# Four stacked graph layers on one core: both graphs' messages in one VectorE instruction, node copies and a positive part on ScalarE

## The chip, the cores and the metric

The kernel runs on one core of a Trainium2 chip. The metric is the device time of one execution in microseconds, lower is better. The engines are named as in the profile: PE is TensorE (PEld its weight loads), DVE is VectorE, ACT is ScalarE, POOL is GpSimd, SP is SyncE. SBUF is the on-chip working memory, PSUM the memory of eight banks per partition that PE writes its results into.

## The reference

There are 128 graphs of 64 nodes, with 128 features per node (`x`) and a 64 x 64 weighted adjacency (`adj`). Four layers follow each other; each adds its result to `x` and normalizes over the features. Layers 0 and 1 are continuous-filter convolutions over edges, layers 2 and 3 are graph convolutions over the whole adjacency.

```python
def ssp(x): return softplus(x) - log(2)

# layer 0 (20 Gaussians); layer 1 is alike with 64 Gaussians and the mask A = adj
f = exp(coeff * (d_ij[..., None] - offsets)**2)        # one row per edge (i, j)
y = x @ w_in2f
W = (ssp(f @ fw1 + fb1) @ fw2 + fb2) * rcut[..., None] # the filter of an edge
agg = einsum('bjf,bijf->bif', y, W)                    # sum of messages per node
x = layernorm(x + ssp(agg @ ow1 + ob1) @ ow2 + ob2)

# layer 2
h = elu(elu(x @ W0 + b0));  h = elu(norm_A @ (h @ W1) + b1)
x = layernorm(x + norm_A @ (h @ W2) + b2)
# layer 3
x = layernorm(x + relu((A_norm @ x) @ W.T + b))
```

## The kernel before

The kernel has a sparse path and a dense one; the sparse one runs here. It sorts the graphs and their nodes by degree, keeps only the nonzero entries of `adj`, and packs them into fixed lists of slots, so that two graphs (a pair) always have the same layout. A prelude of some 85 us does the first part of this; the rest of the packing is spread over the first layer as background work (`early`, `side`), mostly on DVE and POOL.

**The main loop** goes over 64 pairs in layer 0 and 64 in layer 1, each cut into three chunks, so 192 iterations per layer. A chunk holds 316 to 364 slots of each of the two graphs in layer 0 and 380 to 420 in layer 1. For chunk `c` the steps are:

- `filter_in`: PE multiplies the Gaussians `d` with the first filter matrix into the PSUM tile `px` (two banks, one per graph), and ACT takes `h = exp(px + b1)`. `softplus`: ACT takes `h = ln(0.5 h + 0.5)`.
- `gather`: PE multiplies node features `ys` with the one-hot rows `hot` (made on DVE in `one_hot`) into `pg` (two banks); ACT copies it to `g` in SBUF.
- `filter_out`: PE multiplies `h` with the second filter matrix into `pw`, one matmul per graph (each shown as two passes).
- `message`: DVE computes `m = (pw + b2) * g`. After the third chunk of a pair `slot_sums` adds the messages of every node on DVE (lines 1828 and 1832), four such sums at a time in the following iterations.

The loop is skewed by hand: iteration `i` does `filter_in` of chunk `i`, `gather` of chunk `i-1`, and `filter_out` and `message` of chunk `i-2`. The order on each engine is that in which the program issues (`in_order` ties it). Cut down, an iteration is

```python
run(sums, (1, 4, 4)[k]); run(early, ...); run(side, ...)
...
filter_in(c)
gather(c1)
softplus(c)
slot(nodes)                 # one step of node work, every queue in turn
filter_out(c2)
message(c2)
slot(convs[0])
gaussians(n + 1, k)
slot(convs[1])
```

**PSUM** has eight banks: two for `px`, two for `pg`, two for `pw`, and two for node work (`ps_n`, taken in turn by `bank`). `px` and `pg` have one buffer each. `pw` has two buffers of one bank, so that graph 0 of a chunk takes one bank and graph 1 the other, and each bank is free again when its own message has been taken. `g` has two buffers in SBUF, `h` three.

**Node work** is done for groups of four pairs (512 columns), in queues of generators that give one step per `slot`. `node_before` transposes `x` (line 1429), copies it to `xt` (line 1432, DVE), multiplies it with the input matrix, and copies the result to `ys` on ACT. `node_after` multiplies the sums with the first output matrix into `u`, and computes a softplus as `max(u + c1, 0) + ln(0.5 exp(-|u + c1|) + 0.5)`: `na` on ACT (Abs, Exp, Ln) and the positive part `nh` on DVE (line 1558), added on DVE (line 1566); two more matmuls and a normalization follow. `graph_convs` does layers 2 and 3 of a group while layer 1 still runs, with copies from PSUM by `copy` (line 1637: `gxt`, `gy_hw`, `gy_sup`), on DVE, and for the last few groups (`at_end`) on ACT. All activations go by the helper `act` (line 950).

Of the kernel before, what the change touches and what calls it, by code (L numbers as in the profile page):

```python
# [12 lines left out]
F32 = mybir.dt.float32  # L13
AF = mybir.ActivationFunctionType
ALU = mybir.AluOpType
AX = mybir.AxisListType
PSUM = bass.MemoryType.PSUM
DRAM = bass.MemoryType.DRAM

P = 128  # L20
# [581 lines left out]
def sparse_stack(ctx: ExitStack, tc: tile.TileContext, t: dict, out: bass.AP, flag):  # L602
# [11 lines left out]
    nc = tc.nc  # L614
# [155 lines left out]
    for b in range(2):  # L770
        for k in range(3):
            at = slice(A * b + NG0 * k, A * b + NG0 * (k + 1))
            nc.scalar.dma_start(fw1[at, k, :], t["L0_gnn_fw1"])
        at = slice(A * b, A * b + 3 * NG0)
# [101 lines left out]
    with (  # L876
# [31 lines left out]
        to = const.tile([NB, 1], U32, name="graph_to")  # L908
# [18 lines left out]
    node = ctx.enter_context(tc.tile_pool(name="snode", bufs=2))  # L927
    ps_x = ctx.enter_context(tc.tile_pool(name="sps_x", bufs=1, space=PSUM))
    ps_g = ctx.enter_context(tc.tile_pool(name="sps_g", bufs=1, space=PSUM))
    ps_w = ctx.enter_context(tc.tile_pool(name="sps_w", bufs=2, space=PSUM))  # L930


    compacting = ctx.enter_context(ExitStack())
# [5 lines left out]
    def act(out_, in_, func, **kw):  # L939
        nonlocal fence, latest, kind  # L940
        now = func == AF.Sin
        if kind is None or now != kind:
            fence = latest
            if not now:
                ctx_ = tc.issue_after(fence.ins) if fence is not None else nullcontext()
                with ctx_:
                    fence = nc.scalar.preload_act_table_set("natural_log_exp_and_others")
            kind = now
        with tc.issue_after(fence.ins) if fence is not None else nullcontext():
            latest = nc.scalar.activation(out_, in_, func, **kw)  # L950
        return latest
# [407 lines left out]
    g = {}  # L1359
# [12 lines left out]
    def bank(name, n=GS):  # L1372
        ps = ps_n.tile([P, 512], F32, tag="n", name=name)[:, 0 : n * P]
        return ps, ps.rearrange("p (s c) -> p s c", s=n)

    def by_pair(v):
        return v.rearrange("p (s c) -> p s c", c=P)
# [11 lines left out]
    def once(name, n, q):  # L1389

        if n < GS and rings:
            return tiled(name, n, q)
        return node.tile([P, GS * P], F32, tag=name, name=f"{name}_{q}", bufs=1)[:, 0 : n * P]
# [27 lines left out]
    def node_before(layer, q):  # L1421

        w = layers[layer]
        name = f"{layer}_{q}"
        xs = x_all[:, GROUPS[layer][q], :]
        n = xs.shape[1]
        flat, ps = bank(f"xT_{name}", n)
        for s in range(n):
            nc.tensor.transpose(ps[:, s, :], xs[:, s, :], ident)
        yield True  # L1430
        xt = node.tile([P, 512], F32, tag="xt", name=f"xt_{name}", bufs=1)[:, 0 : n * P]
        nc.vector.tensor_copy(xt, flat)

        nc.gpsimd.tensor_tensor(xs, xs, w["c2"].unsqueeze(1).to_broadcast([P, n, C]), ALU.add)
        yield
        flat, ps = bank(f"y_{name}", n)
        for s in range(n):
            nc.tensor.matmul(
                ps[:, s, :], lhsT=xt[:, s * P : (s + 1) * P], rhs=w["win"], start=True, stop=True
            )  # L1440
        yield True
        y = node.tile([P, n, C], F32, tag=f"y{n}", name=f"ys_{name}", bufs={GS: 3, 2: 1, 1: 2}[n])
        act(y, ps, AF.Copy)
        feats[layer, q] = y
        yield


    w = layers[0]
# [4 lines left out]
    u = ps_n.tile([P, 512], F32, tag="n", name="zero_x")  # L1453
# [4 lines left out]
    u = ps_n.tile([P, 512], F32, tag="n", name="zero_w")  # L1458
# [42 lines left out]
    def zero_share(q, agg):  # L1501

        n = agg.shape[1]
        rows = zero_rows.pop(q)
        for b in range(2):
            at = slice(b * A, (b + 1) * A)
            nc.vector.tensor_scalar(zblk[at, :, at], rows[at], 0.0, None, ALU.is_equal)
        yield
        _, ps = bank(f"zT_{q}", n)
        for s in range(n):  # L1510
            nc.tensor.transpose(ps[:, s, :], zblk[:, s, :], ident)
        yield True
        zt = by_pair(once("zt", n, q))
        act(zt, ps, AF.Copy)
        yield
        _, ps = bank(f"zs_{q}", n)
        y = feats[0, q]
        for s in range(n):
            nc.tensor.matmul(ps[:, s, :], lhsT=y[:, s, :], rhs=zt[:, s, :], start=True, stop=True)
        yield True  # L1520
        nc.vector.scalar_tensor_tensor(agg, ps, zero_filter, agg, ALU.mult, ALU.add)
        yield
# [15 lines left out]
    def node_after(layer, q, agg):  # L1538


        w = layers[layer]
        name = f"{layer}_{q}"
        n = agg.shape[1]
        codes = node_codes.pop((layer, q))
        if layer == 0:
            yield from zero_share(q, agg)
        elif n == GS:
            yield
        u, _ = bank(f"u_{name}", n)
        nc.tensor.matmul(  # L1550
            u, lhsT=w["o1"], rhs=agg.rearrange("f s r -> f (s r)"), start=True, stop=True
        )
        yield True
        a = once("na", n, q)
        act(a, u, AF.Abs, bias=w["c1"])
        act(a, a, AF.Exp, scale=-1.0)
        h = once("nh", n, q)
        nc.vector.tensor_scalar(h, u, w["c1"], 0.0, ALU.add, ALU.max)
        yield
        act(a, a, AF.Ln, scale=0.5, bias=half)  # L1560

        back = once("bk", n, q)
        nc.vector.tensor_scalar(back, codes, row[:, 0:1], None, ALU.is_equal)
        back = by_pair(back)
        yield
        nc.vector.tensor_add(h, h, a)
        yield
        _, ps = bank(f"o_{name}", n)
        for s in range(n):
            nc.tensor.matmul(  # L1570
                ps[:, s, :], lhsT=h[:, s * P : (s + 1) * P], rhs=w["o2"], start=True, stop=True
            )
        yield True
        o = by_pair(once("no", n, q))
        act(o, ps, AF.Copy)
        yield
        _, ps = bank(f"back_{name}", n)
        for s in range(n):
            nc.tensor.matmul(ps[:, s, :], lhsT=back[:, s, :], rhs=o[:, s, :], start=True, stop=True)
        yield True  # L1580
        y = by_pair(once("ny", n, q))
        xs = x_all[:, GROUPS[layer][q], :]
        nc.vector.tensor_add(y, ps, xs)
        yield
        yield from layernorm(y, xs, n, name)
        if layer == 1:
            if n < GS:
                yield from graph_convs(q)
            else:
                convs[q % 2].append(graph_convs(q))  # L1590
# [40 lines left out]

    def copy(to, ps, q):

        if q in at_end:
            act(to, ps, AF.Copy)
        else:
            nc.vector.tensor_copy(to, ps)

    normals = {}

# [11 lines left out]
    def graph_convs(q):  # L1652
# [5 lines left out]
        def times(name, lhs, rhs):  # L1658

            _, ps = bank(f"{name}_{q}", n)  # L1660
            for s in range(n):
                nc.tensor.matmul(ps[:, s, :], lhsT=lhs(s), rhs=rhs(s), start=True, stop=True)
            yield True
            y = by_pair(tiled(f"gy_{name}", n, q))
            copy(y, ps, q)
            yield
            return y
# [102 lines left out]
        act(c["h"], c["h"], AF.Ln, scale=0.5, bias=half)  # L1770

    def filter_out(c):
        c["pw"] = []
        for b in range(2):
            ps = ps_w.tile([P, 512], F32, tag="w", name=f"pw_{c['id']}_{b}")
            nc.tensor.matmul(  # L1776
                ps[:, 0 : c["size"]], lhsT=c["w"]["w2"], rhs=c["h"][:, b, :], start=True, stop=True
            )
            c["pw"].append(ps)

    def gather(c):

# [14 lines left out]
    def message(c):  # L1797
        n, k, size = c["n"], c["k"], c["size"]
        if k == 0:
            m = work.tile([P, 2 * MAX_SLOTS], F32, tag="m", name=f"m_{n}")  # L1800
            messages[n] = m[:, 0 : 6 * size].rearrange("f (b k) -> f b k", b=2)
        at = slice(k * size, (k + 1) * size)
        for b in range(2):
            nc.vector.scalar_tensor_tensor(  # L1804
                messages[n][:, b, at], c["pw"][b][:, 0:size], c["w"]["b2"], c["g"][:, b, :],
                ALU.add, ALU.mult,
            )
        if k == 2:
            sums.append(slot_sums(c, messages.pop(n)))

# [31 lines left out]
    at_end = range(NP // GS - 2, len(GROUPS[1]))  # L1842
    last = {q: deque() for q in small_groups}
    stores = deque()
    slot_data, messages, aggs = {}, {}, {}
# [61 lines left out]
    for i in range(3 * N + 2):  # L1907
        n, k = divmod(i, 3)
        c, c1, c2 = None, *past
# [19 lines left out]
        if n < N:  # L1929
            layer, p = pair_at(n)  # L1930
            q = next(q for q, group in enumerate(GROUPS[layer]) if group.start <= p < group.stop)
            c = dict(
                id=f"{n}_{k}", n=n, k=k, s=p - GROUPS[layer][q].start, at=(layer, q), w=layers[layer],
                size=CHUNKS[layer][p // 8],
            )
# [24 lines left out]
        if c2 is not None:  # L1960
            filter_out(c2)
            message(c2)
# [61 lines left out]
```

## Time and profile before

| | |
|---|---|
| median of 3 runs | 1656.86 us (1652.58 to 1659.53) |
| the profiled execution | 1684.44 us |
| its span, first to last instruction | 1682.6 us |
| PE busy | 1474.7 us (88%), 6813 matmul passes |
| DVE busy | 1481.3 us (88%), 4032 instructions |
| ACT busy | 1279.8 us (76%), 1723 instructions |
| POOL busy | 738.2 us (44%), 1180 instructions |
| mean granted clock of PE | 0.961 |

A row of the profile's groups names the line, the engine, the operation, what it writes and reads (`out<-in`), shapes, the count, then the busy time and the mean duration of one, then the engine's idle time just before such instructions and what ended it. A row of waits names who waited for whom, then the total in us, the number of waits and the longest. Layer 0's loop runs from about 95 to 803 us, layer 1's from 803 to about 1610 us, and then a tail of node work for the last groups.

### The profile page before, as it was taken

What the parts mean: (1) busy time and instruction counts of PE and PEld (TensorE: products, weight loads), DVE (VectorE), ACT (ScalarE), POOL (GpSimd) and SP (SyncE); (2) the same over time, 40 slices, a digit from 0 to 9 for tenths busy, and PEclk for the clock granted to TensorE, in tenths of its full rate; (3) what the DMA queues carried; (4) which work ended last, traced back from release to release, by engine and by line L of the source; (5) the groups of instructions that cost most, each with busy time, mean ns of one, the idle gap of its engine ahead of it and who ended that gap; (6) DMA issues with size and microseconds to landing.
All of it is one profiled execution on the core that took longest, in us unless ns stands there. A gap on an engine that the chain in (4) does not pass through costs nothing.

```text
span 1682.6 us, 24560 instructions
## 1 busy us (share of the span) xinstructions
PE 1474.7 (88%) x6813; PEld 816.6 (49%) x6813; DVE 1481.3 (88%) x4032; ACT 1279.8 (76%) x1723; POOL 738.2 (44%) x1180
## 2 busy tenths in 40 slices
PE   0177898999989989998999999999999999998976
PEld 0133454444545545555445555555555555554544
DVE  6677999999998999999888989999999989898874
ACT  1166797878878878887999878888888888787742
POOL 2325155454554533443422355445455335454444
PEclk9999999999999999998999999999999999999975
DMA  7644364545545454444665555555555544466100
GB/s 243 187 113 112 93 142 119 136 121 134 129 108 123 112 136 111 117 114 116 154 154 134 132 118 134 140 121 127 135 122 126 133 119 111 112 141 138 43 8 22
DMA packets 122294, 205.70 MB, mean 122 GB/s; under 512 B 47957, under 2 KB 80035, under 8 KB 121507
## 3 DMA queue, kind: packets, MB, share of 16 engines
q1 hardware_dynamic: 110784, 187.61, 46.1%
q0 software_dynamic: 6576, 14.99, 2.7%
q10 hardware_dynamic: 4786, 1.43, 0.4%
q8 instruction: 57, 0.93, 0.2%
q14 instruction: 91, 0.74, 0.2%
HBM read 185.29 MB, written 18.64 MB: 121 GB/s over the span
## 4 chain that ended last, share of the span: by engine, by line
DVE 32%; PE 25%; DMA 12%; ACT 11%; POOL 9%; issue 7%; SPq 3%; another core or an unknown queue 0%; ACTq 0%; DVEq 0%; POOLq 0%
DVE m L1804 9%; PE pw L1776 9%; DMA out_dram<-gz,at_row 6%; PE px L1762 6%; ACT h L950 5%; DVE agg L1828 5%; PE pg L1789 4%; DVE hot L1750 4%; POOL gz L1413 2%; POOL x_all L1413 2%; SPq L1289 2%; DVE at L1178 2%; ACT g L950 2%; ACT d L950 2%; POOL rs L1408 2%
## 5 line engine op out<-in xcount | busy, mean ns | idle before, releaser
L950 ACT ACTIVATE g<-pg 128x672 f32<-128x672 f32 (+12 forms) x384 | 302.4, 788 | 69.1 <-DVE m L1804 53.8
L950 ACT ACTIVATE h<-h,half 128x672 f32<-128x672 f32 (+13 forms) x385 | 351.4, 913 | 0.1
L1828 DVE TENSOR_REDUCE agg<-m 128x16 f32<-128x240 f32 (+13 forms) x896 | 326.0, 413 | 2.4
L1789 PE MATMUL pg<-hot,ys 64*128 64x336 f32 (+12 forms) x1536 | 316.9, 489 | 10.1 <-DVE hot L1750 7.5
L1776 PE MATMUL pw<-h,w_L_gnn_W2T 128*128 128x420 f32 (+5 forms) x768 | 305.8, 521 | 1.5 <-DVE m L1804 1.5
L1776 PE MATMUL pw<-h,w_L_gnn_fw 128*128 128x336 f32 (+6 forms) x768 | 267.9, 472 | 37.5 <-DVE m L1804 31.8
L950 ACT ACTIVATE h<-px,c_L_gnn_b 128x840 f32<-128x840 f32 (+5 forms) x192 | 178.2, 928 | 120.0 <-PE px L1762 117.2
L1804 DVE SCALAR_TENSOR_TENSOR m<-pw,c_L_gnn_b,g 128x420 f32<-128x420 f32 (+5 forms) x384 | 227.2, 628 | 26.3 <-PE pw L1776 18.4
L1804 DVE SCALAR_TENSOR_TENSOR m<-pw,c_L_gnn_fb,g 128x336 f32<-128x336 f32 (+6 forms) x384 | 202.0, 568 | 26.8 <-PE pw L1776 10.2
L1762 PE MATMUL px<-d,fw 64*128 64x336 f32 (+6 forms) x768 | 169.5, 518 | 54.1 <-DMA d<-d_dram 32.0
L950 ACT ACTIVATE h<-px,c_L_gnn_fb 128x672 f32<-128x672 f32 (+6 forms) x192 | 158.5, 825 | 67.1 <-PE px L1762 50.5
L1789 PEld LDWEIGHTS pg<-hot,ys 64*128 64x128 f32 x1536 | 149.4, 192 | 117.0 <-issue 25.0
L1776 PEld LDWEIGHTS pw<-h,w_L_gnn_fw 128*128 128x128 f32 x768 | 134.3, 194 | 132.4 <-DVE m L1804 74.0
L1776 PEld LDWEIGHTS pw<-h,w_L_gnn_W2T 128*128 128x128 f32 x768 | 134.2, 193 | 130.2 <-issue 30.8
L1750 DVE SCALAR_TENSOR_TENSOR hot<-j,row,w 128x1212 f32<-128x1212 bf16 (+12 forms) x128 | 179.0, 1398 | 9.1 <-DMA w<-w_dram 9.1
L1762 PE MATMUL px<-d,w1t 64*128 64x420 f32 (+5 forms) x768 | 184.1, 557 | 0.1
L1407 POOL TENSOR_SCALAR rs<-mv 128x4 f32<-128x4 f32 x61 | 23.8, 390 | 271.3 <-DVE mv L1401 269.6
L950 ACT ACTIVATE d<-d,neg_off 128x1212 f32<-128x1212 f32 (+12 forms) x128 | 119.4, 933 | 26.0 <-DMA d<-d_dram 13.1
L1762 PEld LDWEIGHTS px<-d,fw 64*128 64x128 f32 x768 | 60.4, 191 | 147.0 <-issue 55.0
L1029 POOL DMA_INDIRECT rows<-comb,goes x64 | 71.4, 1115 | 99.9 <-DMA rows<-comb,goes 71.0
L1413 POOL TENSOR_SCALAR x_all<-ny,mv,rs 128x128 f32<-128x128 f32 x124 | 104.0, 847 | 3.3
L1029 POOL DMA_INDIRECT out_dram<-gz,at_row x56 | 70.4, 1256 | 53.2 <-DMA out_dram<-gz,at_row 40.6
(267 smaller groups left out, 2240.9 us busy)
## 6 DMA issues: line engine op xcount, KB each, us to landing
d<-d_dram SPq DMA_DIRECT2D x32, 315.0 KB
w<-w_dram SPq DMA_DIRECT2D x32, 315.0 KB
d<-d_dram SPq DMA_DIRECT2D x32, 303.0 KB
w<-w_dram SPq DMA_DIRECT2D x32, 303.0 KB
w<-w_dram SPq DMA_DIRECT2D x32, 252.0 KB
j<-j_dram SPq DMA_DIRECT2D x32, 157.5 KB
j<-j_dram SPq DMA_DIRECT2D x32, 151.5 KB
d<-d_dram SPq DMA_DIRECT2D x16, 300.0 KB
```

The lines of the kernel that those rows point to most:

```text
L950: latest = nc.scalar.activation(out_, in_, func, **kw)
L1029: nc.gpsimd.indirect_dma_start(out=into, out_offset=bass.IndirectOffsetOnAxis(ap=at, axis=0), in_=rows, in_offset=None,)
L1178: nc.vector.max_index(out=at[:, r, cut], in_max=top[:, r, cut], in_values=av[:, r, :])
L1289: (engine if name == "d" else nc.sync).dma_start(to, dram_ap(slots[layer, name][s], first, [[0, to.shape[0]], [1, n]]))
L1408: nc.gpsimd.tensor_tensor(rstd, rstd, neg_half[:, 0:n], ALU.pow)
L1413: (nc.gpsimd if n == GS else nc.vector).tensor_scalar(dst[:, s, :], y[:, s, :], mv[:, s, 0:1], rstd[:, s : s + 1], ALU.subtract, ALU.mult,)
L1750: nc.vector.scalar_tensor_tensor(hots[n][:, 0:size], j[:, 0:size], near, wt[:, 0:size], ALU.is_equal, ALU.mult)
L1762: nc.tensor.matmul(ps[:, b, 0:n], lhsT=w1, rhs=d[rows, col : col + n], start=True, stop=True)
L1776: nc.tensor.matmul(ps[:, 0 : c["size"]], lhsT=c["w"]["w2"], rhs=c["h"][:, b, :], start=True, stop=True)
L1789: nc.tensor.matmul(ps[:, b, 0:n], lhsT=y[rows, :], rhs=hots[c["n"]][rows, at], start=True, stop=True,)
L1804: nc.vector.scalar_tensor_tensor(messages[n][:, b, at], c["pw"][b][:, 0:size], c["w"]["b2"], c["g"][:, b, :], ALU.add, ALU.mult,)
L1828: nc.vector.tensor_reduce(av[:, :, :, r], both, AX.X, ALU.add)
```

## The change

Three things are changed.

- `filter_out` takes one PSUM tile of two banks for both graphs instead of two tiles of one bank, and the pool has one such buffer; the two matmuls stay. `message` does both graphs with one DVE instruction over the two banks. The banks in use are as many as before.
- `node_before` copies `xt` on ACT, and `copy` always uses ACT (the test on `at_end` goes).
- In `node_after` the positive part `nh` is a Relu with bias on ACT, issued between the Exp and the Ln of `na`.

```diff
-    ps_w = ctx.enter_context(tc.tile_pool(name="sps_w", bufs=2, space=PSUM))
+    ps_w = ctx.enter_context(tc.tile_pool(name="sps_w", bufs=1, space=PSUM))
@@ node_before
-        nc.vector.tensor_copy(xt, flat)
+        act(xt, flat, AF.Copy)
@@ node_after
         act(a, u, AF.Abs, bias=w["c1"])
         act(a, a, AF.Exp, scale=-1.0)
         h = once("nh", n, q)
-        nc.vector.tensor_scalar(h, u, w["c1"], 0.0, ALU.add, ALU.max)
+        act(h, u, AF.Relu, bias=w["c1"])
         yield
         act(a, a, AF.Ln, scale=0.5, bias=half)
@@ copy
-        if q in at_end:
-            act(to, ps, AF.Copy)
-        else:
-            nc.vector.tensor_copy(to, ps)
+        act(to, ps, AF.Copy)
@@ filter_out
-        c["pw"] = []
+        ps = ps_w.tile([P, 2, 512], F32, tag="w", name=f"pw_{c['id']}")
+        c["pw"] = ps[:, :, 0 : c["size"]]
         for b in range(2):
-            ps = ps_w.tile([P, 512], F32, tag="w", name=f"pw_{c['id']}_{b}")
             nc.tensor.matmul(
-                ps[:, 0 : c["size"]], lhsT=c["w"]["w2"], rhs=c["h"][:, b, :], start=True, stop=True
+                c["pw"][:, b, :], lhsT=c["w"]["w2"], rhs=c["h"][:, b, :], start=True, stop=True
             )
-            c["pw"].append(ps)
@@ message
-        for b in range(2):
-            nc.vector.scalar_tensor_tensor(
-                messages[n][:, b, at], c["pw"][b][:, 0:size], c["w"]["b2"], c["g"][:, b, :],
-                ALU.add, ALU.mult,
-            )
+        nc.vector.scalar_tensor_tensor(
+            messages[n][:, :, at], c["pw"], c["w"]["b2"], c["g"], ALU.add, ALU.mult
+        )
```

In the prelude the order of a few instructions changes with it: small operations on DVE that rank the nodes for layer 1 (lines 811 to 841) move ahead of the first sort, and on ACT the first `xt` stands ahead of one DMA (line 1063).

## The prediction

> **What bounds the kernel now.** I read the page first (engine shares), then the windows by stage, then the waits of TensorE (PE) and of the message line in each stage, and last the timeline of a few iterations. The time is set by a loop of 384 chunk iterations, 192 for each filter layer, and the two layers differ.
>
> From the windows (start:end, length, then busy us and instructions of PE, its weight loads, VectorE (DVE), ScalarE (ACT), GpSimd; granted clock; DMA):
>
> ```profile
> 95.00:803.00 708.00, 629.25 (x2951) 339.96 (x2952) 658.28 (x2061) 558.67 (x814) 317.13 (x525) 0.97 0.49 121
> 803.00:1550.00 747.00, 729.45 (x3392) 402.63 (x3390) 678.45 (x1521) 638.30 (x772) 330.79 (x376) 0.99 0.55 129
> 800.00:850.00 50.00, 49.99 (x210) 23.53 (x210) 44.45 (x96) 49.52 (x59) 25.32 (x25) 1.00 0.71 159
> 850.00:900.00 50.00, 49.51 (x208) 23.51 (x206) 43.65 (x89) 47.74 (x57) 10.10 (x14) 1.00 0.63 141
> ```
>
> In layer 0 (first row) DVE is busy 93%, PE 89%, ACT 79%. In layer 1 PE is busy 98%, DVE 91%, ACT 85%; just after the change of layers PE and ACT are both full. So layer 0 has time to win (79 us of PE idle in 708), layer 1 hardly any (18 of 747). What ends PE's idle time in layer 0 (waits of PE: total us, times, longest):
>
> ```profile
> PE pw L1776 <- DVE m L1804: 31.8, 34, 3.1
> PE px L1762 <- ACT h L950: 19.1, 12, 4.0
> PE pg L1789 <- DVE hot L1750: 7.5, 12, 2.1
> ```
>
> and ACT's largest wait there:
>
> ```profile
> ACT g L950 <- DVE m L1804: 52.8, 64, 2.3
> ```
>
> The second filter matmul `pw` needs a PSUM bank that the last chunk's message on DVE must free, and ACT's copy `g` needs a buffer that a message frees. DVE runs late and holds both. The timeline (start, us) shows one case:
>
> ```profile
> 618.03 1.04 DVE L1804 SCALAR_TENSOR_TENSOR m<-pw,c_L_gnn_fb,g 128x336 f32<-128x336 f32 x2
> ...
> 618.65 1.40 PE L1776 MATMUL pw<-h,w_L_gnn_fw 128*128 128x336 f32 x4 [0.69 <-DVE m L1804]
> ```
>
> `pw` starts 0.62 us after the first message starts, while the second still runs: each graph has its own bank. Over all chunk pairs of the timeline `pw` starts within 0.1 us of the first message's end in 57 of 191 cases in layer 0 and 4 of 192 in layer 1.
>
> [...] 96 messages of 336 elements are busy 50.0 us, 521 ns each, 96 of 404 are busy 56.9 us, 593 ns each, so 1.06 ns an element and about 165 ns fixed. [...] DVE's `nh` waits for ACT's `na`, which reads the same bank, 42.5 us in 23 waits.
>
> **The change part by part.**
>
> *One message for two.* 384 instructions go, each with some 165 ns fixed: DVE loses 0.17 x 384 = 65 us, 33 in layer 0. Against that, two waits get coarser. The merged message needs all of `pw`, not its first half, and `pw` needs the whole message gone. A message of 336 elements has a duration of 562 ns; one of 672 at 1.06 ns more an element is 0.92 us, so a gated `pw` starts 0.35 us later after the same message start. If all 57 cases stayed gated that is 20 us in layer 0. On DVE, the message starts before `pw` is complete in 51 of 192 chunks in layer 0 and 83 in layer 1; there DVE now idles for up to half a `pw` (0.65 to 0.75 us). Queued behind it are the slot sums, the one-hot product and node steps; PE waits for the latter two. In layer 1 DVE has slack for this (91% before, below 80% after), and the median distance from the second message's end to the next `pw` is 1.1 us there.
>
> *Node copies to ACT.* DVE loses `xt` 34 (21.8 us), `gy_hw`, `gy_sup` and `gxt` 56 (19.1 + 9.6 + 9.4 us). ACT gets 34 + 56; its own copy from PSUM of this size, `ys`, takes 594 ns: 19 + 33 = 52 us.
>
> *Positive part to ACT.* DVE loses `nh` 34 (24.4 us) and the 42.5 us idle before it. ACT gets 34 at the price of `na`'s first step on the same input, 684 to 704 ns: 23 us. No extra table loads: Copy and Relu already run between Exp and Ln here. In the tail this step moves into ACT's chain between Exp and Ln: three small groups at 0.37 to 0.47 us, +1 us. No instruction on PE, GpSimd or SyncE and no DMA is added or moved past another, so their cost is nil apart from the waits.
>
> *Start.* The rank computation on DVE moves ahead of the first sort. One DMA on ACT's queue now waits behind the first `xt` (some 2.5 us) and DVE runs some 2 us of small operations earlier; against that go the 4.2 us of them between the first matmuls (91.9 to 96.05). Net -1 us.
>
> So DVE loses about 150 us of 1481 and ACT gains 75. Layer 0: DVE 658 - 33 - 22 = 603 (85%), ACT 559 + 20 = 579 (82%). Layer 1: ACT gets 51 copies, 14 `xt` and 14 `nh`, 48 us: 687 (92%).
>
> *Sum, layer 0.* Idle of PE that leads back to DVE: 31.8 + 7.5 + about 4 of small waits, and 19.1 by way of ACT: 62 us. There are 34 stalls of `pw`, one in 5.6 chunks, while DVE gains 0.28 us a chunk, 1.6 us between two stalls; but earliness is lost whenever DVE catches up with PE. I choose half of the 62: -31. I also choose about half of the 57 gated cases to stay, and add some that were just covered: +14. Net -17.
>
> *Sum, layer 1.* PE is full, so no gain but part of `gx`, whose 12.5 us wait for GpSimd's normalization leads back to DVE: -3. From 800 to 900 us ACT has 97.3 us of work and gets 4: over full, +3 with its waits. Later ACT is 92% full, and the PSUM tiles `px` and `pg` have one buffer each; +3. Net +3.
>
> With start -1 and tail +1 to 2: -17 + 3 - 1 + 2 = **-13 us**. The profiled execution took 1684.4 us (span 1682.6); the median of the runs is 1656.9, 1.6% less, with the same program. I take the difference over: **1644 us**.
>
> **The rivals.** A, the sum above: 1644, between 1633 and 1653.
>
> B, the coarser handshake gives back what DVE saves. For: `pw` to message to `pw` is a chain of 1.3 + 0.92 + waits = 2.4 us of a 3.7 us iteration, where a half was 1.3. Against: layer 1 has 1.1 us of distance. Then layer 0 gives nothing, 1657 with layer 1's few us either way.
>
> C, ACT becomes the bound of layer 1, slower. For: ACT 92% beside PE 98%, in order, with single buffers `px` and `pg`; every ACT instruction ahead of `h` delays the next `px`. Against: at 800 to 850 us both were full and PE did not stall, and `px` ends 3.3 us before the next one starts while its `h` takes 0.9. It decides once ACT is more than 2.4 us late. If two thirds of ACT's 48 us land on PE, +32, less 13: 1676.
>
> D, DVE's relief lands fully in layer 0: PE's own 629 us plus some 15 of start-up is the limit, -50 with the rest: 1610. Against: one message buffer ties DVE to PE.
>
> That the merged message is no cheaper (each bank paying its own fixed cost) is a further way to B; ACT already reads two banks in one instruction (`g`, 128x672 in 0.79 us).
>
> **How the numbers follow.** A measurement of this kernel tells about 0.5% (8 us) from no change. A 0.44, nearly all faster; B 0.26, same; C 0.22, slower; D 0.08, faster. Faster 0.50, same 0.28, slower 0.22. The range leaves out the ends of C and D: 1620 to 1674.
>
> **What would show it.** DVE busy near 1330 us and ACT near 1355; messages 384 with 0.85 to 1.1 us each; the wait of `nh` for `na` gone. In layer 0 PE's idle before `pw` well below 31.8 us and ACT's wait for messages below 52.8. Wrong if `pw`'s waits for messages grow (B), or if `px` or `pg` wait for ACT in layer 1, where those waits are absent from PE's list now (C).

## The result: no difference, and the profile after

| | before | after |
|---|---|---|
| median of 20 runs each, us | 1655.0 (1645.8 to 1667.0) | 1655.6 (1646.7 to 1665.1) |
| ratio, with its 95% interval | | 1.0005 (0.9987 to 1.0023) |
| the profiled execution's span, us | 1682.6 | 1655.7 |
| mean granted clock of PE | 0.961 | 0.971 |

The forecast was 1644 us, faster by 13 us. The time is that of before to 0.2%. The two profiled spans must not be set against each other: the one of before, on which the prediction worked, was 28 us longer than its kernel's median. A second profile of the kernel before (span 1649.4 us) lies under its median; what is called "before" below is this second profile.

The engine shares of the changed kernel show that the work moved off DVE:

```profile
PE 1459.7 (88%) x6813; PEld 813.1 (49%) x6813; DVE 1362.2 (82%) x3524; ACT 1335.4 (81%) x1847; POOL 745.8 (45%) x1180
```

DVE lost 119 us (1481.3 to 1362.2) and 508 instructions (384 messages, 124 node steps); ACT gained 55.6 us and those 124. In the costliest groups the merged messages, layer 1 first:

```profile
L1799 DVE SCALAR_TENSOR_TENSOR m<-pw,c_L_gnn_b,g 128x840 f32<-128x840 f32 (+5 forms) x192 | 201.3, 1049 | 134.7 <-PE pw L1773 120.5
L1799 DVE SCALAR_TENSOR_TENSOR m<-pw,c_L_gnn_fb,g 128x672 f32<-128x672 f32 (+6 forms) x192 | 176.9, 921 | 61.7 <-PE pw L1773 54.8
```

They take 378.2 us instead of 429.2. New is the idle time behind the second bar: DVE now waits 175 us in all for `pw`, where it waited for some 25 before. Two things are in this: a message now needs the whole of `pw`, and DVE, with less to do, is there sooner (with the merged message alone the wait is 92 us). The windows of the two loops, from the first message of a layer to the next layer's (layer 0, layer 1; columns as ahead of the prediction), first before, in its second profile:

```profile
90.00:784.00 694.00, 624.62 (x2952) 338.97 (x2953) 657.12 (x2056) 558.24 (x814) 322.43 (x526) 0.98 0.47 123
784.00:1585.00 801.00, 775.42 (x3640) 430.31 (x3639) 731.64 (x1653) 681.34 (x827) 363.53 (x422) 0.99 0.52 125
```

and after:

```profile
89.00:769.00 680.00, 620.89 (x2953) 339.84 (x2953) 617.14 (x1834) 572.08 (x846) 322.37 (x527) 0.98 0.49 126
769.00:1591.00 822.00, 781.90 (x3637) 432.45 (x3638) 657.25 (x1371) 723.36 (x916) 366.04 (x421) 0.99 0.51 122
```

Layer 0 became 14 us shorter (694 to 680), near the forecast's 17. Layer 1 became 21 us longer (801 to 822; in a second profile of the changed kernel 813), where +3 was forecast. Some of that spread is PE's clock: the first profile after has four dips of the granted clock from 1208 us on (0.79 in the 8 us from 1208), the last beginning at 1318 us, the second none there, and PE is busy 782 us in one and 777 us in the other for the same work. In layer 1 PE's idle time grew from 25.6 to 40.1 us (36 in the second profile) although DVE and ACT are both less than 90% busy (80% and 88%). PE's waits in the window 803 to 1550 us name what is new:

```profile
PE gx L1670 <- POOL x_all L1413: 12.0, 30, 0.7
PE o L1711 <- ACT nh L950: 8.5, 6, 1.7
PE hw L1659 <- ACT nh L950: 5.0, 6, 0.9
PE px L1759 <- ACT h L950: 1.0, 1, 1.0
```

`o` and `hw` are matmuls of layers 3 and 2, run as node work beside layer 1. They wait for the new positive part `nh` on ACT, since `nh` is the last reader of `u`, and `u` holds one of the two PSUM banks that all node work shares. In the second profile of before (765 to 1560 us) the same two were small:

```profile
PE gx L1673 <- POOL x_all L1413: 8.6, 21, 0.5
...
PE o L1714 <- DVE nh L1558: 2.1, 4, 0.7
...
PE hw L1662 <- DVE nh L1558: 0.3, 1, 0.3
```

In layer 0 the waits that the prediction counted on are these, first before (90 to 784 us):

```profile
PE px L1762 <- ACT h L950: 21.1, 11, 8.0
ACT g L950 <- DVE m L1804: 56.5, 69, 2.3
```

and after (89 to 769 us):

```profile
PE pw L1773 <- DVE m L1799: 27.5, 36, 2.0
PE px L1759 <- ACT h L950: 22.8, 13, 7.5
ACT g L950 <- DVE m L1799: 18.1, 35, 1.9
```

The line of `pw` before, 33.4 us, stands below with those of the experiments.

### The profile page after: what moved, and what is told of

Its sections match the earlier page's. It is cut to its first block, busy times and chain, and to the rows that moved or that the text cites. A ratio compares the mean times of both kernels' runs of the same rounds, so it can differ in the third digit from the quotient of the medians.

```text
span 1655.7 us, 24261 instructions
## 1 busy us (share of the span) xinstructions
PE 1459.7 (88%) x6813; PEld 813.1 (49%) x6813; DVE 1362.2 (82%) x3524; ACT 1335.4 (81%) x1847; POOL 745.8 (45%) x1180
## 5 line engine op out<-in xcount | busy, mean ns | idle before, releaser
L950 ACT ACTIVATE g<-pg 128x672 f32<-128x672 f32 (+12 forms) x384 | 303.9, 791 | 27.2 <-DVE m L1799 18.1
L1785 PE MATMUL pg<-hot,ys 64*128 64x336 f32 (+12 forms) x1536 | 311.7, 482 | 3.2 <-DVE hot L1747 3.2
L1799 DVE SCALAR_TENSOR_TENSOR m<-pw,c_L_gnn_b,g 128x840 f32<-128x840 f32 (+5 forms) x192 | 201.3, 1049 | 134.7 <-PE pw L1773 120.5
L1773 PE MATMUL pw<-h,w_L_gnn_fw 128*128 128x336 f32 (+6 forms) x768 | 268.9, 474 | 27.8 <-DVE m L1799 27.5
L1799 DVE SCALAR_TENSOR_TENSOR m<-pw,c_L_gnn_fb,g 128x672 f32<-128x672 f32 (+6 forms) x192 | 176.9, 921 | 61.7 <-PE pw L1773 54.8
L1407 POOL TENSOR_SCALAR rs<-mv 128x4 f32<-128x4 f32 x61 | 22.8, 374 | 281.2 <-DVE mv L1401 279.5
L1759 PEld LDWEIGHTS px<-d,w1t 64*128 64x128 f32 x768 | 58.3, 186 | 66.5 <-ACT h L950 31.3
```

Of the source, the lines that this page charges most:

```text
L1407: nc.gpsimd.tensor_scalar(rstd, mv[:, :, 1], LN_EPS, None, ALU.add)
L1759: nc.tensor.matmul(ps[:, b, 0:n], lhsT=w1, rhs=d[rows, col : col + n], start=True, stop=True)
L1773: nc.tensor.matmul(c["pw"][:, b, :], lhsT=c["w"]["w2"], rhs=c["h"][:, b, :], start=True, stop=True)
L1785: nc.tensor.matmul(ps[:, b, 0:n], lhsT=y[rows, :], rhs=hots[c["n"]][rows, at], start=True, stop=True,)
L1799: nc.vector.scalar_tensor_tensor(messages[n][:, :, at], c["pw"], c["w"]["b2"], c["g"], ALU.add, ALU.mult)
```

## The experiments

Each ratio is to runs of the kernel before on the same chip. Three chips were used at first, on which that kernel takes 1654.2 to 1654.9 us, so that runs on them are set beside each other below. Called "the bank theory" (N in the expectations) is: the time is lost where PE, in order and 97% busy in layer 1 (775 of 801 us before), waits for a node bank that `u` holds until its last reader is done. Its rival is that ACT's load is what costs (rival C of the prediction, A in the expectations). For the message the rival is that the coarser handshake, one message that waits for the whole of `pw` and a `pw` that waits for the whole message, costs what the instruction saves (rival B, H in the expectations).

### The noise, and the parts one by one

The kernel before, unchanged:

> The kernel before, profiled once more. Its first profile took 1684 us where the runs have a median of 1655, and its first 16 chunks took 76 us where the changed kernel's took 65, with 13.7 us of half clock among them. If the sum went wrong because that profile was an unusual one, this one shows a layer 0 of about 685 to 695 us instead of 707, with PE's wait of pw for messages below 25 us. If the first profile was typical, layer 0 is again 700 us or more. Ratio 1.000.

1654.72 against 1654.24 us, 0.9999 (0.9981 to 1.0017): a difference of 0.3% is real here. Layer 0 took 694 us, as expected of an unusual first profile, but `pw` waited 33.4 us, not below 25: the waits were usual.

The merged message alone (the hunks of the pool, `filter_out` and `message`):

> The merged message alone, copies and positive part as before. Theory H (the coarser handshake gives back what the merged instruction saves): same, 1650 to 1660, DVE busy 65 us less, pw's waits for messages in layer 0 as long as before or longer. Theory A (ACT gave it back in layer 1): faster by 8 to 12 us. Theory P (PE's own work bounds both layers, DVE time buys nothing): same, and pw's waits shrink.

1655.54 us, 0.9999 (0.9981 to 1.0017): nothing, as H expects. The steps moved to ACT alone (the hunks of `xt`, `nh` and `copy`), with two messages and two banks:

> The node copies and the positive part on ScalarE, messages as before with one bank for each graph. Theory H: faster by 5 to 12 us, since DVE is relieved of 84 us and the handshake stays fine. Theory A: same or slower, up to 1665, with px or pg waiting for ACT in layer 1. Theory P: same, within 3 us.

1648.56 us, 0.9969 (0.9952 to 0.9986): 5.7 us faster.

### What the merged message gives and takes

The handshake alone: one tile of two banks as in the change, but still two messages.

```diff
-    ps_w = ctx.enter_context(tc.tile_pool(name="sps_w", bufs=2, space=PSUM))
+    ps_w = ctx.enter_context(tc.tile_pool(name="sps_w", bufs=1, space=PSUM))
@@ filter_out
...
+        ps = ps_w.tile([P, 2, 512], F32, tag="w", name=f"pw_{c['id']}")
+        c["pw"] = ps[:, :, 0 : c["size"]]
@@ message
-                messages[n][:, b, at], c["pw"][b][:, 0:size], c["w"]["b2"], c["g"][:, b, :],
+                messages[n][:, b, at], c["pw"][:, b, :], c["w"]["b2"], c["g"][:, b, :],
```

> One PSUM tile of two banks as in the change, but still two message instructions: the coarser handshake without its saving (DVE's time as before). Theory H: slower by 10 to 25 us, mostly in layer 0, with more gated pw. Theory A and P: slower by less than 5 us.

1668.83 us, 1.0089 (1.0054 to 1.0124): 14.6 us slower. And DVE time alone: the kernel before at the old handshake, with every slot sum leaving out the last quarter of its slots. It was meant to take from DVE what the merged message saves.

```diff
@@ slot_sums
-            one = v[:, :, base[r] : base[r] + caps[r]]
+            one = v[:, :, base[r] : base[r] + caps[r] * 3 // 4]
...
-            nc.vector.tensor_reduce(av[:, :, h, 0], v[:, :, at : at + cap], AX.X, ALU.add)
+            nc.vector.tensor_reduce(av[:, :, h, 0], v[:, :, at : at + cap * 3 // 4], AX.X, ALU.add)
```

> The kernel before, with every slot sum taken over the first three quarters of its slots only (a part of the computation is left out): some 0.18 us of DVE less per chunk, about what the merged message saves, with the fine handshake kept. Theory H (DVE's time is worth something, the handshake took it): faster by 8 to 15 us, nearly all in layer 0. Theory P (PE's own work bounds, DVE's time is worth nothing): same.

1640.17 us, 0.9915 (0.9898 to 0.9932): 14.2 us faster. How much DVE was relieved, first here, then with the merged message alone:

```profile
PE 1457.5 (89%) x6813; PEld 810.2 (49%) x6813; DVE 1409.3 (86%) x4032; ACT 1276.0 (78%) x1723; POOL 743.1 (45%) x1180
PE 1459.8 (88%) x6813; PEld 815.2 (49%) x6813; DVE 1433.9 (87%) x3648; ACT 1280.2 (77%) x1723; POOL 741.9 (45%) x1180
```

Before, DVE was busy 1479.2 us. So the sums took away 70 us and the merged message only 45; an estimate in proportion makes the latter worth some 9 us. So time on DVE is worth something, the coarse handshake costs something, and the merged message, which has both, comes out at nil. How large each of the two is inside it was not measured: the handshake was tried with two messages, one behind the other (1.04 us for the two of 336 elements in the prediction's timeline), and the merged one is shorter (0.91 us). The waits of layer 0 follow. Before (90 to 784 us):

```profile
PE pw L1776 <- DVE m L1804: 33.4, 39, 1.5
```

with the coarse handshake alone (90 to 796 us):

```profile
PE pw L1776 <- DVE m L1803: 54.0, 55, 2.2
```

with DVE relieved alone (90 to 770 us):

```profile
PE pw L1776 <- DVE m L1804: 23.3, 34, 1.6
```

and with the merged message alone (90 to 778 us):

```profile
PE pw L1776 <- DVE m L1802: 40.1, 49, 2.0
```

The coarse handshake adds 20.6 us to PE's wait, the relief takes 10.1 away, and the merged message leaves 6.7 more than before.

### The steps moved to ACT, apart

The positive part alone (the hunk of `nh`), the copies alone (those of `xt` and `copy`), and the merged message with the copies:

> The positive part alone on ScalarE. Theory N (it holds the PSUM bank of u for Abs, Exp and Relu, and o and hw of layers 2 and 3 wait for that bank): slower by 4 to 10 us, with o and hw waiting some 15 us for nh in layer 1. Theory A (ACT's load alone costs time): slower by less than 3 us and the waits spread over px and pg. Theory D (relief of DVE wins): faster by 2 to 5 us.

> The node copies alone on ScalarE, fine handshake, positive part on DVE. Theory N: faster by 8 to 14 us, more than with the positive part moved too (act_only gained 5 us). Theory A: faster by 5 us or less, as act_only or worse.

> The change without the move of the positive part: merged message and node copies on ScalarE. If nh in the ACT queue is what layer 1 lost: faster than the change and before by 5 to 10 us. If the coarser handshake loses in layer 1 as well: same as before, within 3 us.

They gave 1648.27 us, 0.9953 (0.9935 to 0.9972); 1644.29 us, 0.9939 (0.9925 to 0.9953); 1644.83 us, 0.9946 (0.9932 to 0.9961). The whole change, run once more:

> The changed kernel, profiled once more beside its variants: 1652 to 1658. If layer 1 of its first profile (823 us from the first to the last message) was an unusual one, this one has 810 us or less; if it is the loss that cancels layer 0's gain, 815 us or more, with o and hw waiting some 15 us for nh.

1651.53 us, 0.9983 (0.9965 to 1.0001). And the merged message with the positive part, without the copies:

> The merged message with the positive part on ScalarE, copies on DVE. If the parts only clash through the bank that nh holds behind the copies in ACT's queue: faster than before by 3 to 8 us, as nh_only. If the merged message and the moved positive part clash directly: same as before or slower.

1650.38 us, 0.9977 (0.9961 to 0.9993). So the copies are worth 10 us and the positive part 6, each on its own, but the two together less than the copies alone: adding the positive part to the merged message and the copies turns 0.9946 into 0.9983. The bank theory had expected the positive part alone to be slower by 4 to 10 us. This failed: `o` and `hw` waited 8.2 us for the bank, and the kernel was faster all the same, so what DVE is spared weighs more there. A layer 1 of 813 us in the second profile of the change lies between the two cases that its expectation names, and decides nothing.

PE's granted clock is a rival for part of these gains. Its mean over the runs was 0.972 for the kernel before on all three chips, and 0.9747 with the copies, 0.9775 with the merged message and the copies, 0.9752 with all steps on ACT, 0.9743 with the whole change run once more. Over the 43 runs of the kernel before on the chip of the last, 0.001 more of clock went with 1.1 us less. By this estimate 3 to 6 of the copies' 10 us go with the clock, and 3 of the 3.4 of the whole change; whether the kernels cause the difference was not tested.

### What is lost when both are moved

If the bank is the cause, `u` must be given up sooner with the same work on ACT. The Relu is put ahead of the Exp, which doesn't read `u`: in the changed kernel, and in the one with two messages.

```diff
         act(a, u, AF.Abs, bias=w["c1"])
-        act(a, a, AF.Exp, scale=-1.0)
         h = once("nh", n, q)
         act(h, u, AF.Relu, bias=w["c1"])
+        act(a, a, AF.Exp, scale=-1.0)
```

> The changed kernel with Relu issued ahead of Exp, so that the PSUM bank of u is free one ACT instruction (0.61 us) earlier. Theory N (the bank that nh holds on ACT is what layer 1 lost): faster than the changed kernel by 4 to 9 us, with the waits of o and hw for nh below 9 us instead of 14.8. Theory A (ACT's load in layer 1 lost it): same as the changed kernel, since ACT does as much.

> Copies and positive part on ScalarE with Relu ahead of Exp, messages as before with one bank for each graph. Theory N: faster than before by 10 to 15 us (act_only gained 5, copies_only 10). Theory A: as act_only, 5 us faster than before.

1638.56 us, 0.9905 (0.9875 to 0.9935), and 1639.01 us, 0.9910 (0.9882 to 0.9938), where the same kernels with the Exp first stand at 0.9983 and 0.9969. One exchange of two neighbouring instructions, with the same ones on every engine, is worth 13 us, for which 4 to 9 were expected, and 9.5 us, and the changed kernel with it is 16 us faster than before: the sum of the parts. These two are the fastest versions found; the merged message makes no difference between them. The clock is no rival here: the means are 0.9758 for 0.9743 in the first pair, an estimated 1.6 of the 13 us, and lower with Relu first in the second (0.9723 for 0.9752). PE's waits in layer 1 (765 to 1560 us), first the change in its second profile:

```profile
PE o L1711 <- ACT nh L950: 8.2, 6, 1.7
PE hw L1659 <- ACT nh L950: 6.2, 7, 1.3
```

then with Relu ahead of Exp:

```profile
PE o L1711 <- ACT nh L950: 4.6, 6, 1.0
PE hw L1659 <- ACT nh L950: 1.7, 6, 0.6
```

8.1 us of waiting go from these two lines. The two profiled spans are only 6.6 us apart (1641.7 and 1635.1 us), since the profiled execution of the change was the fastest of its 22 runs; so where the rest of the 13 us between the medians lies, these profiles can't show. Between kernels with two messages the lines fall by 8.9 us, PE's idle time in layer 1 by 9.0, for 9.5 us of time.

One such wait in the timeline of the changed kernel (start and duration, us; in brackets the idle time before it and what ended it):

```profile
912.06 0.60 ACT L950 ACTIVATE gy_sup<-sup 128x512 f32<-128x512 f32 x1
...
912.17 1.12 PE L1550 MATMUL u<-agg,w_L_gnn_Wd1T 128*128 128x512 f32 x2
912.54 0.95 ACT L950 ACTIVATE h<-px,c_L_gnn_b 128x808 f32<-128x808 f32 x1
...
913.36 0.86 ACT L950 ACTIVATE g<-pg 128x808 f32<-128x808 f32 x1
914.08 1.00 ACT L950 ACTIVATE h<-h,half 128x808 f32<-128x808 f32 x1
...
914.94 0.72 ACT L950 ACTIVATE na<-u,c_L_gnn_bd 128x512 f32<-128x512 f32 x1
915.69 0.63 ACT L950 ACTIVATE na<-na 128x512 f32<-128x512 f32 x1
...
916.23 0.67 ACT L950 ACTIVATE nh<-u,c_L_gnn_bd 128x512 f32<-128x512 f32 x1
...
916.95 1.16 PE L1659 MATMUL hw<-w_L_gnn_W,er 128*128 128x128 f32 x8 [0.89 <-ACT nh L950]
...
918.04 0.61 PE L1759 MATMUL px<-d,w1t 64*128 64x404 f32 x2
```

`u` is complete at 913.29. ACT, busy with a copy of the node work (`gy_sup`, one of those that the change moved) and the chunk's `h`, `g` and Ln, comes to the Abs at 914.94; the Exp follows, then the Relu, which ends at 916.90. `hw` needs the bank and starts 0.05 us later, and the next chunk's `px` stands behind it on PE. Without the Exp in between (0.63 us) `u` would be free some 0.6 us sooner. Of the 3.6 us that `u` is held, 1.65 pass before ACT begins. This is the part that the copies add to: in layer 1 it is 1.1 us (median) before and with the positive part alone, and 1.55 with the copies on ACT too; the Exp and the Relu then come on top.

### Two doses more

On another chip, where the kernel before takes 1670.33 us, `u` was given up at once, with more work for ACT: it copies `u` to SBUF first and takes Abs and Relu from there, 34 instructions more.

```diff
         a = once("na", n, q)
-        act(a, u, AF.Abs, bias=w["c1"])
-        act(a, a, AF.Exp, scale=-1.0)
         h = once("nh", n, q)
-        act(h, u, AF.Relu, bias=w["c1"])
+        act(h, u, AF.Copy)
+        act(a, h, AF.Abs, bias=w["c1"])
+        act(a, a, AF.Exp, scale=-1.0)
+        act(h, h, AF.Relu, bias=w["c1"])
```

> The changed kernel with u first copied to SBUF by ScalarE, and Abs, Exp and Relu on the copy: ScalarE does 34 instructions more (some 20 us), but the bank of u is free after one of them. Theory N (the held bank is the loss): faster than the changed kernel by 5 to 12 us in spite of the added work, o and hw waiting less than 5 us. Theory A (ScalarE's load is the loss): slower than the changed kernel by 5 us or more.

1653.75 us, 0.9914 (0.9881 to 0.9946). The change was not run on this chip; its ratios elsewhere are 1.0005 and 0.9983. ACT has more to do than in the change (1354 us busy for 1335), the granted clock is no higher than before (0.968 for 0.969), and the kernel is faster. This speaks against ACT's load as the cause. PE's waits (770 to 1560 us) for the bank are all but gone, those for ACT's `h` grew from 1.4 us:

```profile
PE px L1760 <- ACT h L950: 3.5, 5, 1.0
...
PE o L1712 <- ACT nh L950: 0.3, 1, 0.3
```

The other way, the Relu was put behind the Ln, a step of the queue later:

```diff
-        act(h, u, AF.Relu, bias=w["c1"])
         yield
         act(a, a, AF.Ln, scale=0.5, bias=half)
+        act(h, u, AF.Relu, bias=w["c1"])
```

> The changed kernel with Relu behind Ln, one step of the node queue later: the same work on ScalarE, the bank of u held longer. Theory N: slower than the changed kernel by 8 us or more, with the waits of o and hw above 20 us. Theory A: same as the changed kernel.

1670.05 us, 0.9992 (0.9975 to 1.0009): within the ratios of the change, and not 8 us slower, so the forecast of the bank theory failed here. From the end of the matmul to the end of the last reader `u` is now held 9.4 us (median in layer 1; 3.5 in the change, 2.9 with Relu ahead of Exp, 2.2 with the copy, 2.6 before), yet PE waits no longer. The waits (770 to 1560 us) have other names:

```profile
PE o L1711 <- ACT gy_hw L950: 8.0, 6, 1.6
PE hw L1659 <- DVE gz L1719: 6.0, 7, 0.9
```

The timeline of one case shows why:

```profile
935.97 0.69 DVE L1719 SCALAR_TENSOR_TENSOR gz<-o,x_all 128x512 f32<-128x512 f32 x1 [0.35 <-PE o L1716]
936.71 1.16 PE L1659 MATMUL hw<-w_L_gnn_W,er 128*128 128x128 f32 x8 [0.86 <-DVE gz L1719]
...
941.85 0.68 ACT L950 ACTIVATE nh<-u,c_L_gnn_bd 128x512 f32<-128x512 f32 x1
```

`hw` is written 5 us before the Relu reads `u`, so it is not in the bank of `u`: with the Relu a step later the other bank is given to it, the one that `o` filled and `gz` empties. That bank comes free about as late (936.66, 0.86 us of waiting, beside 0.89 in the change). 14.0 us of waits in place of 14.4, and the time of the change. What failed is the step from a longer hold to a longer wait, where the bank asked for is no longer the one that is held. PE's idle time in layer 1, 38 us, is again that of the change.

The other versions, put in order of the time that `u` is held, show the step from hold to wait holding there (layer 1, one profile each; PE's idle time is from the first message to the last):

| version | `u` held, us (median) | `o` and `hw` wait for its last reader, us | PE idle, us |
|---|---|---|---|
| `u` copied first | 2.2 | 0.3 | 28 |
| before | 2.6 | 2.4 | 26 |
| Relu first, two messages | 2.9 | 5.9 | 25 |
| Relu first, changed kernel | 2.9 | 6.3 | 30 |
| positive part alone | 3.1 | 8.2 | 31 |
| copies alone | 3.1 | 9.1 | 31 |
| both, two messages | 3.5 | 14.8 | 34 |
| the change, second profile | 3.5 | 14.4 | 36 |

From 2.6 to 3.5 us of holding, the waits grow from 2.4 to 14.4 us. They are a part of the time and not the whole of it: the copies alone wait more than before and are 10 us faster.

## Why the prediction was wrong

By its own steps:

- **384 merged messages save 0.17 us each, 65 us: too large.** 429.2 - 378.2 = 51 us, 0.13 each. The duration, 0.92 us forecast for 672 elements, came (0.91). The prediction's own figures already gave the smaller saving: two messages of 336 are busy 2 x 521 ns, and 1.04 - 0.92 is 0.12 us. A message alone takes 0.56 us, but two in a row took 1.04 in its timeline and not 1.12: there the second started before the first ended, and that saving is gone once they are one.
- **The coarser handshake, +14 in layer 0: of that order, but in the wrong balance.** With two messages it costs 14.6 us (layer 0: 706 us for 694); with one it was not measured apart. The merged message by itself is nil. Rival B held for this part. It did not hold for the whole, for the copies pay by themselves.
- **Half of the 62 us of stalls go: near in sum, wrong in place, and so in part luck.** Layer 0 gained 14 us of the 17: 10 of PE's idle time (69.4 to 59.1 us), the rest in its busy time. `pw`'s wait only fell from 33.4 to 27.5 us. ACT's wait to write `g` fell from 56.5 to 18.1, but the wait of `px` for ACT, 19.1 of the 62, which was to follow from it, did not fall (21.1 to 22.8). "Well below 31.8" was not met, "below 52.8" was.
- **Copies +52 us on ACT, positive part +23: right as durations, too large by 20 as busy time.** The moved steps last 53 and 22 us on ACT, but its busy time grew by 55.6 us. Neighbours overlap in the trace: in the timeline above `gy_sup` ends at 912.66, and the next step has begun at 912.54. On DVE, too, some 68 us went besides the messages where 84 were counted. No table load was added, as forecast: 18 before and after, 1.28 us each. The error that sank the forecast is not this one.
- **Layer 1, +3: the step that failed.** The Relu was costed as 23 us of an engine with room, and its wait for ACT on DVE (42.5 us) as gone. But the last reader of `u` went behind the Exp in the queue of an engine that the copies had just filled. "No instruction on PE ... is added or moved past another, so their cost is nil apart from the waits" left exactly these waits out: PE waits for the node bank 14.4 us in place of 2.4, on an engine with 26 us of idle time in the layer. So layer 1 got 12 to 21 us longer for the +3 of the forecast. Relu ahead of Exp wins back 13 us by itself; that this equals the predicted gain is chance.
- **Rival C, `px` and `pg` waiting for ACT: did not come.** `px` waits 1.4 us for ACT's `h` in layer 1, and a version with 34 more instructions on ACT is faster. It looked for ACT's load in the main chain; what came was ACT's lateness at a bank of the node work.
- **Start -1, tail +1 to 2: as small as forecast,** as far as single profiles tell: the first message came at 89 us for 90, and the stretch behind the last one took 63.4 us in both. Rival D, DVE's relief landing in full, did not come: 27.5 us of `pw`'s wait stayed.
- **The difference of 1.6% between profile and median carried over: no cause of the error,** though the execution read was an unusually long one: the two waits the sum rests on were nearly the same in the second profile (33.4 for 31.8, 56.5 for 52.8).

What stays open: why the lone gains of copies (10 us) and positive part (6) add to 16 once the Relu goes first, though layer 0 takes 684 us with the copies, 683 with the positive part and 680 with both, and the bank waits of each alone (8.2 and 9.1 us) are above before's 2.4. Layer 1 in single profiles spreads by some 10 us, too much to settle it, and the granted clock, higher with the copies, is not ruled out as a part of their lone gain.

## What to carry to other kernels

When a step that reads PSUM is moved to another engine, cost not only its duration but the moment at which the last reader lets the bank go, and look at who claims the bank next: here `u` was held for 3.5 us instead of 2.6, and `o` and `hw` waited 14.4 us for its last reader instead of 2.4. In the new queue put the steps that read the bank first and those that work in SBUF behind them; here Relu ahead of Exp was worth 13 us. One instruction over two banks took 0.13 us less than two here, and made two handshakes into one: with a single buffer the two can cancel, as here (0.9999), so weigh each by itself. A test that frees an engine has to free it by the same amount as the change (here it took away 70 us for the message's 45): read the busy time before the two are set against each other. Where one engine is 98% busy in order, as PE in the prediction's window of layer 1, a wait of 1 us that comes a dozen times is the size of the whole gain: 14.4 us in 13 waits here, where 13 were forecast.

## What the runs showed of the hardware

An instruction on DVE over two PSUM banks at once took 909 ns for 128x672 and 1091 ns for 128x840, where one over a single bank took 562 ns for 128x336 and 651 for 128x420; at the 1.06 ns an element that these two give, an estimate for the longer ones is 918 and 1096 ns, so no penalty for the second bank is visible, but merging saved only 0.13 us against two. Neighbouring instructions on ACT overlapped in the trace: moved steps that last 75 us added 55.6 us to its busy time. The same Relu with bias on 128x512 elements from PSUM took 0.67 us on ACT, where DVE's add and max took 0.75. The same program's profiled spans lay 33 us apart (1682.6 and 1649.4 us), while its medians over 12 to 44 runs on three chips agreed within 0.05% (1654.2 to 1654.9 us); on a fourth chip it was 1% higher (1670.3 us).
